# Where the closing steps of the first two elements' attention stand in the issue grid of a four-layer kernel

## Chip, core and metric

The kernel runs on one core of one Trainium2 chip. The metric is the device time of one execution in microseconds (us). Three runs of the kernel before the change took 1100.51, 1100.62 and 1100.92 us.

Five engines are named as the profile names them: PE (matrix engine; PEld is its weight load), DVE (vector engine), ACT (activation engine), POOL (general engine) and SP (which issues all the transfers here). Each engine takes its instructions strictly in the order in which the program lists them, and waits at the first one whose inputs or buffer are not ready.

## What is computed

Four batch elements x[b] of 512 rows by 512 columns go through two decoder layers with gates; g are scalars.

```
x = x + tanh(g_xattn[0]) * wkv(layernorm(x), ctx)        # a scan over the 512 rows, per column
x = x + tanh(g_ffn[0])   * ffn(layernorm(x))             # 512 -> 2048 -> 512, one-bit weights, 8-bit groups
x = x + tanh(g_xattn[1]) * attention(layernorm(x), ctx)  # 16 heads of 32, int8 projections
x = x + tanh(g_ffn[1])   * ternary(layernorm(x))         # rms norm * gamma, 8-bit rows, ternary weight
```

The attention ends, per row, with `out = qdq(o) @ qdq(wp).T + bp`, where qdq rounds a row to 8 bits by its largest magnitude. The ternary layer takes the row's statistics again, scales by gamma, rounds the row to 8 bits by its largest magnitude, and multiplies by a 512x512 ternary matrix. Both are row-wise, so each of the four tiles of 128 rows can be done by itself.

## The kernel before, in words

Rows are cut in four tiles of 128 (t = 0 to 3). Elements are b = 0 to 3 (NB = 4). The four layers of different elements overlap in a pipeline: while element b is in its FFN, element b-1 is in its attention, element b+1 in its scan layer, and the tail of element b-2 (end of attention, ternary layer) is done beside them.

**The order is made by a grid.** Each layer is a Python generator that stops at `yield` after every step. `line(gen, (start, end, steps), ...)` gives it places: a part of n steps is spread evenly from start to end. `run` (L1192, with `place` at L1180) always takes the step with the smallest place next. One element is 1.0 wide and has SLOTS = 17 places, one for each unit of the FFN and a spare; below, "place 6.5" means 6.5/17 of an element behind the beginning of the FFN of element b+2. A line with `aside=True` is put at the integer part of its place plus 0.8. On PE the steps keep this order (`in_turn`, `next_turn`, L147 to L160). On the other engines and SP a scheduler orders the instructions from it, and moves many of them.

**The unit.** One place holds one FFN unit of a row tile (two groups of eight matmuls to `ff_hp`, eight to `ff_acc`, four transposes to `tp_ps`) and one attention unit of a head pair (four `s_ps` matmuls, transposes `pt_ps`, the values `o_ps`, `ot_ps`). On DVE a unit has four row maxima (`at_nm`, L939), the gating (L738, L742), the 8-bit groups (L214, L668, L670, L672), the second halves (L689) and the collection of the head outputs (L991). A chunk of the scan layer adds, every second place, three scans (L591, L621, L626), two reciprocals (L632) and products on POOL (L600, L622, L627, L628, L633, L634).

**What the change moves.** For one row tile, `project_out` (L1008) has three steps: DVE takes the row's largest magnitude (L214) and its scale (L218, L219), and ACT rounds the row (L223); PE transposes it (`qr_ps`, L165) and ACT copies it to `at_oqT` (L230); PE multiplies (`p_ps`, four matmuls), DVE scales the result to `at_y` (L1027), and POOL adds it to `xb` (L1028). The four tiles run staggered by one step, so they take six steps. The ternary layer (L1162) begins with the statistics of all four tiles (L191 to L203, with POOL's power in L180). Per tile, it then centres and scales the row on POOL (`tf_xn`, L211 and L1134), takes its largest magnitude and four short scales on DVE (L214, L1137 to L1145), rounds on ACT (L223), transposes (`qr_ps`, `tf_xT`), multiplies (`f_ps`) and adds on DVE (L1158), and SP stores the rows (L1159): seven staggered steps.

**Buffers in the way.** `at_row` is a ring of three row buffers (ROWS = 3) shared by `at_xn`, `at_q`, `at_half`, `at_y` and `tf_xn`. `m` is three PSUM banks shared by `qr_ps`, `p_ps`, `f_ps`, `pt_ps`, `ot_ps`, `o_ps`, `q_ps`, `tp_ps` and `wy_ps`; `hp` is three banks for `s_ps` and `ff_hp`. The head outputs `at_o` of an element have one buffer, which the next element's attention takes over: its first write (L991) must wait until the last transpose of the element before has read it.

## Time and profile before

| what | value |
|---|---|
| median of three runs | 1100.62 us (1100.51 to 1100.92) |
| the profiled execution: its own time | 1100.92 us |
| the profiled execution: span from first to last instruction | 1099.1 us |
| busy in the span: PE / DVE / ACT / POOL | 939.7 / 831.4 / 726.0 / 314.1 us |
| mean granted PE clock | 0.963 |
| first `ff_acc` of the stretch in which the closing steps of b = 0 stand, and of that of b = 1 | 591.73 and 810.96 us |

The profiled execution's time is 1.8 us more than its span, and 0.3 us more than the median. A unit can be followed in the trace by its group of eight `ff_acc` matmuls; the time from one group to the next is called a unit below. In a row of instructions the columns are start, length, engine, line and operation, and in brackets the idle time of the engine before it and who ended it. A row of a table by stretches gives the stretch and its length, and then, for each engine, its busy time and number of instructions, and at the end the granted PE clock, the transfer engines' busy share and GB/s.

### The profile page before, as it was taken

Reading aid. Unit: us, or ns where it says so; the run is one execution under the profiler, and the core shown is the slowest. Engines: PE = TensorE matmul, PEld = TensorE weight load, DVE = VectorE, ACT = ScalarE, POOL = GpSimd, SP = SyncE. Lnnn points to the kernel's source line nnn. Section 1 sums busy time; section 2 is a strip of 40 time slices with the busy share of each in tenths; the row PEclk is TensorE's granted clock in tenths of the full one; section 3 lists DMA queues with packets and bytes.
Section 4 is the critical chain, followed back from the end, with each engine's and each line's share of the span. In section 5 each row is a group of like instructions: output and inputs, shape, how many; then the busy total and the mean of one; then the engine's idle time right before and its main releaser. Section 6 shows DMA issues by size and latency. Waiting matters only on the chain.

```text
span 1099.1 us, 17965 instructions
## 1 busy us (share of the span) xinstructions
PE 939.7 (85%) x6380; PEld 678.8 (62%) x6380; DVE 831.4 (76%) x1600; ACT 726.0 (66%) x1490; POOL 314.1 (29%) x311
## 2 busy tenths in 40 slices
PE   4879997998888878889998787999998999878885
PEld 2335564565557666667776465777777777656652
DVE  4976548757676789997669988877697765679977
ACT  6656755567345676667767667677685666977863
POOL 3831104422323153531215546422123321100000
PEclk8889999999998999999999999999999999989998
DMA  8178945454344673744755544566455653343411
GB/s 287 39 257 326 323 170 187 147 216 171 136 134 148 233 234 112 252 134 144 230 190 189 168 164 145 172 216 187 173 200 169 208 192 106 83 149 107 116 49 39
DMA packets 85674, 189.68 MB, mean 173 GB/s; under 512 B 12241, under 2 KB 36817, under 8 KB 74577
## 3 DMA queue, kind: packets, MB, share of 16 engines
q1 hardware_dynamic: 85584, 188.53, 51.6%
q8 instruction: 51, 0.84, 0.3%
q14 instruction: 39, 0.31, 0.1%
HBM read 148.65 MB, written 39.85 MB: 171 GB/s over the span
## 4 chain that ended last, share of the span: by engine, by line
PE 45%; DVE 24%; ACT 15%; POOL 7%; issue 7%; DMA 2%; SPq 0%; POOLq 0%; ACTq 0%; DVEq 0%
PE ff_hp L162 14%; PE ff_acc L162 6%; PE pt_ps L165 5%; PE o_ps L162 4%; PE s_ps L162 4%; ACT at_P L941 3%; DVE wk_q L632 3%; PE v_ps L162 3%; ACT at_PT L961 2%; DVE at_nm L939 2%; PE k_ps L162 2%; PE tp_ps L165 2%; DVE wk_p L626 2%; PE qr_ps L165 2%; DVE qg_i L672 1%
## 5 line engine op out<-in xcount | busy, mean ns | idle before, releaser
L162 PE MATMUL ff_hp<-wT,xp 128*128 128x512 f32 x1024 | 270.0, 407 | 3.8 <-ACT at_P L941 2.1
L162 PEld LDWEIGHTS ff_hp<-wT,xp 128*128 128x128 f32 x1024 | 194.2, 193 | 51.3 <-ACT at_P L941 3.8
L941 ACT ACTIVATE at_P<-s_ps,at_nm 128x512 f32<-128x512 f32 x256 | 174.4, 689 | 73.9 <-DVE at_nm L939 70.0
L939 DVE TENSOR_REDUCE at_nm<-s_ps 128x1 f32<-128x512 f32 x256 | 165.5, 676 | 38.0 <-PE s_ps L162 37.3
L677 POOL TENSOR_TENSOR ff_z<-qg_b,qg_s 128x512 f32<-128x512 bf16 x64 | 71.8, 1121 | 334.4 <-ACT qg_b L676 308.3
L165 PE MATMUL pt_ps<-ident,at_P 128*128 128x128 f32 x1024 | 141.1, 278 | 16.4 <-ACT at_os L981 5.4
L961 ACT COPY at_PT<-pt_ps 128x512 f32<-128x512 f32 x224 | 124.3, 595 | 39.6 <-PE pt_ps L165 38.5
L162 PE MATMUL ff_acc<-wT,hr 128*128 128x512 f32 x512 | 137.3, 409 | 4.8 <-ACT hr L688 3.0
L165 PEld LDWEIGHTS pt_ps<-ident,at_P 128*128 128x128 f32 x1024 | 113.2, 140 | 44.4 <-issue 9.1
L162 PE MATMUL s_ps<-at_kR,at_qR 128*128 128x512 f32 x256 | 97.8, 450 | 22.0 <-ACT at_P L941 14.6
L162 PEld LDWEIGHTS ff_acc<-wT,hr 128*128 128x128 f32 x512 | 92.7, 190 | 25.8 <-ACT hr L688 4.0
L737 ACT ACTIVATE ff_z<-ff_hp,coef 128x512 f32<-128x512 f32 x64 | 44.0, 687 | 46.9 <-PE ff_hp L162 44.3
L162 PE MATMUL o_ps<-at_PT,at_V 128*32 128x128 f32 x2048 | 72.2, 279 | 1.3 <-DVE hr L689 0.7
L676 ACT CAST qg_b<-qg_i 128x512 bf16<-128x512 int8 x80 | 49.3, 617 | 31.3 <-DVE qg_i L672 27.4
L742 DVE SCALAR_TENSOR_TENSOR ff_z<-ff_hp,coef,ff_z 128x512 f32<-128x512 f32 x64 | 47.6, 743 | 29.1 <-PE ff_hp L162 29.1
L162 PEld LDWEIGHTS s_ps<-at_kR,at_qR 128*128 128x128 f32 x256 | 45.6, 193 | 38.8 <-ACT at_P L941 23.7
L162 PEld LDWEIGHTS o_ps<-at_PT,at_V 128*32 128x32 f32 x2048 | 53.8, 111 | 23.8 <-issue 11.3
L738 DVE SCALAR_TENSOR_TENSOR ff_z<-ff_z,ff_hp 128x512 f32<-128x512 f32 x64 | 43.4, 678 | 31.4 <-ACT ff_z L737 29.5
L162 PE MATMUL v_ps<-wkvT,cT 128*128 128x512 f32 x128 | 60.9, 622 | 5.7 <-DVE wT L295 2.3
L162 PE MATMUL k_ps<-cT,wkvT 128*128 128x512 f32 x128 | 61.4, 631 | 2.3 <-ACT wk_k L576 1.0
L165 PE MATMUL tp_ps<-ident,ff_z 128*128 128x128 f32 x256 | 40.3, 281 | 23.2 <-ACT at_PT L961 11.0
L632 DVE RECIPROCAL wk_q<-wk_q 128x256 f32<-128x256 f32 x32 | 54.3, 1718 | 1.4 <-POOL wk_p L620 1.4
(178 smaller groups left out, 1664.3 us busy)
## 6 DMA issues: line engine op xcount, KB each, us to landing
wT<-wD SPq DMA_DIRECT2D x72, 1024.0 KB, 5.3
wn<-in_L_ffn_w_dram SPq DMA_DIRECT2D x18, 1024.0 KB, 7.2
at_kR<-kD SPq DMA_DIRECT2D x128, 128.0 KB, 3.0
at_qR<-qD SPq DMA_DIRECT2D x256, 64.0 KB, 2.3
wD<-wT SPq DMA_DIRECT2D x12, 1024.0 KB, 4.2
kD<-k_half SPq DMA_DIRECT2D x16, 512.0 KB, 2.8
qD<-at_half SPq DMA_DIRECT2D x32, 256.0 KB, 2.1
cn<-in_ctx_dram SPq DMA_DIRECT2D x8, 512.0 KB, 6.0
```

What stands on the lines that cost most here:

```text
L162: return in_turn(nc.tensor.matmul(*args, **kwargs))
L165: return in_turn(nc.tensor.transpose(*args))
L626: nc.vector.tensor_tensor_scan(p[:, 1:], A2, E2, 0.0, ALU.mult, ALU.add)
L632: nc.vector.reciprocal(half, half)
L676: nc.scalar.copy(qb, qi)
L677: nc.gpsimd.tensor_tensor(grouped(src), grouped(qb), s.unsqueeze(2).to_broadcast([P, NG, GS]), ALU.mult)
L737: nc.scalar.activation(z, hp, AF.Tanh, scale=coef[:, 0:1])
L738: nc.vector.scalar_tensor_tensor(z, z, 1.0, hp, ALU.add, ALU.mult)
L742: nc.vector.scalar_tensor_tensor(z, hp, coef[:, 1:2], z, ALU.mult, ALU.mult)
L939: nc.vector.tensor_reduce(nm, sp, AX.X, ALU.max, negate=True)
L941: nc.scalar.activation(lanes[k, i, t], sp, AF.Exp, bias=nm, accum_out=sums[k][:, t, i : i + 1],)
L961: made[k] = nc.scalar.copy(dst, blocks(pt))
```

## The change

Two entries of the placing are changed. For every element but b = 2, the six steps that end the attention are spread from `end` to `end + 2.4` places before, and from `end - 0.1` to `end + 3.8` places after. For b = 0 and 1, the seven steps of the ternary layer run from `end + 3` to `end + 8` before, and from `end + 4.1` to `end + 9.1` after.

```diff
             (start, end, 72),
-            (end, end + 2.4 / SLOTS, 6)
+            (end - 0.1 / SLOTS, end + 3.8 / SLOTS, 6)
             if b != NB - 2
             else (end - 0.15 / SLOTS, end + 4.65 / SLOTS, 6),
...
                 late(lambda b=b: ternary_layer(b, xs[b], at)),
-                (end + 3 / SLOTS, end + 8 / SLOTS, 7)
+                (end + 4.1 / SLOTS, end + 9.1 / SLOTS, 7)
                 if b < NB - 2
                 else (end + 4.85 / SLOTS, end + 11.85 / SLOTS, 7),
```

`end` is place 5.95 of the FFN of element b+2. Worked out, the steps stand at these places (the ternary layer's with the rule for `aside`):

| steps | before | after |
|---|---|---|
| end of attention, 6 | 5.95, 6.35, 6.75, 7.15, 7.55, 7.95 | 5.85, 6.5, 7.15, 7.8, 8.45, 9.1 |
| ternary layer, 7 | 8.8, 9.8, 10.8, 11.8, 11.8, 12.8, 13.8 | 10.8, 10.8, 11.8, 12.8, 12.8, 13.8, 14.8 |

For b = 3 nothing else is left to be placed beside these steps. No instruction is added, removed or changed in size.

## Prediction

> **What bounds the kernel here.** I read the table by stretches first, cut at the first `ff_acc` matmul of each unit from place 6.25 on. This is the unit table for the closing steps of b = 0:

> ```profile
> 591.73:613.99 22.26, 16.02 (x104) 11.31 (x105) 20.71 (x33) 16.24 (x33) 14.53 (x13) 0.92 0.73 224
> 613.99:631.92 17.93, 13.60 (x100) 9.86 (x99) 16.96 (x23) 9.88 (x21) 12.16 (x12) 1.00 0.41 146
> 631.92:643.74 11.82, 10.76 (x89) 8.65 (x87) 10.32 (x22) 7.05 (x18) 2.89 (x4) 1.00 0.31 96
> 643.74:659.86 16.12, 12.56 (x88) 9.84 (x87) 14.71 (x30) 11.66 (x22) 8.78 (x8) 0.89 0.58 210
> 659.86:674.58 14.72, 11.20 (x93) 9.09 (x91) 12.99 (x24) 8.97 (x23) 9.74 (x10) 1.00 0.52 163
> 674.58:693.89 19.31, 14.65 (x101) 10.87 (x99) 16.21 (x35) 12.39 (x23) 13.40 (x13) 0.91 0.47 157
> 693.89:706.50 12.61, 11.84 (x96) 9.57 (x95) 11.48 (x24) 9.70 (x25) 3.25 (x3) 1.00 0.33 95
> ```

> Of these 114.8 us PE (first column after the length) is busy 90.6 and DVE (third) 103.4. DVE is the bound, at 90%, and what it lacks, 11.4 us, is waiting. The first two units are long because five of the six closing steps fall into them; the third has no closing step of the attention and takes 11.82.

> The same cut for b = 1, whose neighbour has no scan layer left, shows PE as the bound:

> ```profile
> 810.96:824.20 13.24, 13.24 (x104) 10.21 (x102) 12.93 (x30) 12.28 (x28) 4.81 (x5) 1.00 0.77 266
> 824.20:837.14 12.94, 12.89 (x100) 9.94 (x98) 10.82 (x23) 7.80 (x18) 4.50 (x4) 1.00 0.92 293
> 837.14:850.13 12.99, 10.15 (x84) 8.20 (x83) 9.37 (x26) 7.70 (x21) 4.11 (x4) 1.00 0.07 18
> 871.95:887.53 15.58, 13.07 (x100) 9.77 (x99) 12.63 (x35) 9.09 (x21) 9.82 (x9) 1.00 0.45 138
> ```

> PE idles there only in the last two, 2.84 and 2.51 us. So spreading as such can win nothing: PE's or DVE's work is the same wherever it stands. Only waits can go. DVE's waits between 591.73 and 706.5, longest first:

> ```profile
> DVE tf_s L214 <- POOL tf_xn L1134: 3.4, 3, 1.5
> DVE ln_r L203 <- POOL ln_r L180: 1.8, 2, 1.4
> DVE wk_p L626 <- POOL wk_e L622: 1.4, 2, 0.9
> DVE at_y L1027 <- PE p_ps L162: 1.0, 1, 1.0
> DVE s L191 <- POOL xb L1028: 0.7, 1, 0.7
> ```

> Four of the five are of the moved steps or stand behind them. PE's longest waits in both stretches are effects of a late DVE:

> ```profile
> 609.21 1.11 PE L165 MATMUL qr_ps<-ident,at_o 128*128 128x128 f32 x4 [3.85 <-ACT at_o L223]
> 652.68 1.26 PE L162 MATMUL q_ps<-at_xqT,wqT 128*128 128x512 bf16 x4 [3.56 <-DVE at_o L991]
> 845.36 0.63 PE L165 MATMUL tp_ps<-ident,ff_z 128*128 128x128 f32 x4 [2.84 <-DVE at_o L991]
> ```

> **Part 1, end of attention for b = 0.** The issue order of the changed program puts one closing transposition and product less before the `ff_acc` at 613.99, and two in the unit that had none. In PE's queue the first `qr_ps` now stands behind two `s_ps`, which loses about 0.4 us of cover for the 1.14 us that the second `s_ps` waits at 596.29; DVE's reciprocals (597.39, 3.33 us) end later than that, so it costs nothing. The wait of 3.85 at 609.21 goes, since the row that it transposed is now rounded a unit earlier than needed. What DVE gains of it is only its own two waits, 1.0 (`at_y`) and 0.7 (`s`). One comes new: the last `at_y` (L1027) is now followed after four short rows by the statistics of that tile, which wait for POOL's sum (L1028, 1.29). Queued behind on DVE are the next `ff_acc` result and two row maxima. Sum: -1.7 + 1.3 = **-0.4**. Bounds: -1.7 if other rows fit between, +1.3 if the two old waits only move.

> **Part 2, ternary layer for b = 0.** The wait of L203 on POOL's power (1.4) stays: the order still has both side by side. The three waits on `tf_xn` (3.4) and 0.3 of `at_half` (L895, idle before it at 667.83) belong to a ring: `tf_xn` of tile 0 stands in `at_row` before the rows of the query projection at place 9.75, so the second `at_half` waits until tile 0 is transposed (667.20), POOL's next `tf_xn` waits for L895 (2.12 us idle at 668.75), and DVE waits for POOL at 671.86 (1.47) and 676.21 (0.83). Afterwards the projection's rows come first, and all three `tf_xn` that are queued there follow them; DVE's L214 for tile 0 stands some thirty rows behind L203 instead of five. POOL then needs 3 x (0.77 + 1.28) us while DVE has a scan, two reciprocals (3.3) and six row maxima to do. Sum: **-3.7**. Bounds: 0 (DVE's next row waits instead) to -4.8 (with part of the L622 wait).

> **Part 3, work that leaves the DVE-bound stretch.** Two adds (L1158, 0.73 each) and tile 3's magnitude with four short rows (0.68 + 4 x 0.15) now come behind 706.5: 2.7 us of DVE, at 90% worth 2.4. PE gets with them three transpositions (start to start 0.43) and two products (0.86) in the units of 12.61, 12.83 and 11.39, where it is idle 0.77, 1.13 and 0.22: 3.0 - 2.1 = 0.9 more. Sum: **-1.5**. Bounds: -2.4 to +0.6 (only PE's 3.0 less the 2.4).

> **Part 4, b = 1.** Where PE is full, moving its work one unit on is neutral. The 2.84 wait: DVE waited 1.13 (L203) and 2.27 (L214 behind `tf_xn`) ahead of two row maxima. Now it has 1.2 (statistics behind L1028) and 1.13, and the first `tf_xn` magnitude is a unit later; the matmuls that stand in front (a product, 0.86, and a projection before `tp_ps`) cover some. I leave 1.3 of 2.84: -1.5. The 2.51 at 877 to 882 I leave as they are: the three `tf_xn` chains are as dense as before (POOL 2.05 per tile against 0.9 of DVE between), only a unit earlier, where DVE has more slack (6.60 busy of 10.76) but POOL's queue must first wait for L895.

> **Part 5, a held bank.** `at_o` has one buffer: the next element's first collection (L991) writes it after the last `qr_ps` has read it. Before, that transposition (618.23, and 828.43) came ahead of the first `ot_ps` (620.80, 830.82), so L991 followed at once. Now, in the order, two transpositions come behind `ot_ps`, which keeps its PSUM bank until then, and eight `m` tiles go through two banks. The order shows the consequence: the third `qr_ps` and its product now wait for DVE, that is for the second halves of the `tp_ps` ahead (L689). In b = 1 these ended 2.1 us after their `tp_ps`, with an `at_y` and statistics (1.4) ahead of them that are now gone; I take 1.2 of the 0 to 2.1. In b = 0 I follow PE through the two banks from 612.7 and reach the next `ff_acc` about 4.6 us later than with three, yet still when DVE is ready for it: 0, and 4.6 if DVE were not the later one. Sum with part 4: -1.5 + 1.2 = **-0.3**, from -3.5 to +3.0.

> **Queues passed.** SP: the stores of `out` wait for L1158 (21.5 us in four waits between 570 and 720) with weight loads behind them; two stores now stand together ahead of the load of the last up-weights, which are used some 19 us of PE rows later. Nothing, or one weight load's landing (5.3) if that cover went. POOL: the sums L1028 fall behind products of the scan chunk; their readers are the statistics alone. ACT is busy below 80% in all the units shown but 810.96 (12.28 of 13.24).

> **Ports.** Two of the four L1028 lie beside a lengthened L672 (1.25 and 1.27 against 0.68), the other two beside rows of normal length: 1.2 us of collisions. As many POOL rows run afterwards: I take 0, from -1.2 to +1.2. [...]

> **Sum.** -0.4 - 3.7 - 1.5 - 0.3 = -5.9. Against the profiled execution's 1100.92 (0.3 above the median, inside what repeats differ by) that is **1095.0**. What ends a unit early is kept: nearly everything after 731 is PE-bound with units of 9 to 13 us and no fixed appointments.

> **Rivals.**
> - *The waits move.* POOL's chain for the four ternary tiles is as long as before (8 x about 1 us), and DVE's rows that read it find it late at their new place, so part 2 gives 0 and part 3 half. -0.4 - 0.7 - 0.3 = -1.4: 1099.5. For it: part 4's own case, where the density stays. Against it: DVE's new position, thirty rows behind L203.
> - *The held bank bites (slower).* If DVE turns the two banks over later than PE needs them, the 4.6 of part 5 are on the path in b = 0 and 2.1 in b = 1; it decides as soon as PE's `ff_acc` of place 8.25 ends after DVE wants it, and my margin there is only about 1 us. With half of part 2 and nothing of part 3: +6.7 - 1.9 - 0.4 = +4.4: 1105.3. For it: PE already waits 2.8 us at `tp_ps` behind `at_PT` and 2.8 us at `pt_ps` behind `at_os` in the stretch of b = 0, each for a bank. Against it: there PE is idle 3.5 us per unit, DVE 1.6.
> - *The order doesn't change* is excluded: every engine's list differs in both stretches, and nowhere else.

> **Numbers.** Forecast 0.62, waits move 0.20, held bank 0.18. 0.2% (2.2 us) is about what a measurement of this kernel can tell from no change. Faster by more: 0.61 of the forecast and 0.03 of the first rival, 0.64; within: 0.01, 0.17 and 0.01 of the three, 0.19; slower: 0.17 of the held bank. The range takes the bounds of part 2 to the good side (a further 5 with parts 1 and 4), and to the other goes past the first rival to a held bank that costs half: 1089.5 to 1102.5.

> **What would show it.** Right: no PE wait of 3 us at the `qr_ps` of `at_o`; DVE waits on `tf_xn` of b = 0 under 1 us in all; the stretch from 591.73 to the ninth `ff_acc` after it 5 us shorter; b = 1's stretch within 2 us. Wrong: `tf_s` waits of 3 us again; PE waits at `qr_ps` or `p_ps` on L689 that lengthen the unit at place 7.25; a PE wait at `tp_ps` of 2 us or more near place 9.5 of b = 1.

## The result, and the profile after

The changed kernel takes 1106.26 us (median of four runs, 1105.39 to 1109.16) against 1100.77 us for the kernel before in the same measurement (1100.51 to 1101.92): a ratio of 1.0057, 95% interval 1.0041 to 1.0072. It is slower by 5.5 us where 5.8 us less than the median before were forecast. A second measurement (twelve runs, the last experiment) gives 1.0033, 1.0019 to 1.0046. The profiled execution takes 1106.21 us and has a span of 1104.4 us, 5.3 more than before. Cut at the same `ff_acc` groups, the 5.3 are +0.5 up to 592 (where both kernels issue the same), +1.2 in the ten units of b = 0 (149.77 against 148.55), -0.2 between, +4.1 in the ten units of b = 1 (124.23 against 120.17), and -0.3 behind.

This is the table by units of b = 0 after the change. The first seven rows answer to the seven that the prediction shows; the last three are the units behind them. The last line, from the same table of the kernel before, is the sum of its last three units.

```profile
592.22:610.74 18.52, 13.07 (x95) 9.75 (x97) 18.52 (x29) 13.10 (x29) 12.80 (x12) 1.00 0.69 236
610.74:632.49 21.75, 14.53 (x95) 11.17 (x95) 18.57 (x28) 12.07 (x25) 12.18 (x11) 0.76 0.49 148
632.49:645.58 13.09, 12.82 (x100) 9.88 (x99) 11.88 (x24) 8.64 (x20) 2.64 (x4) 1.00 0.27 92
645.58:660.22 14.64, 12.47 (x87) 9.83 (x87) 12.41 (x24) 9.46 (x18) 6.65 (x7) 0.88 0.49 162
660.22:676.22 16.00, 11.49 (x89) 8.60 (x87) 15.47 (x26) 10.53 (x24) 13.04 (x12) 1.00 0.67 211
676.22:687.64 11.42, 10.55 (x88) 8.61 (x87) 10.07 (x28) 10.36 (x19) 4.73 (x5) 1.00 0.66 224
687.64:705.92 18.28, 13.52 (x104) 10.32 (x103) 16.70 (x30) 11.00 (x26) 12.73 (x11) 1.00 0.29 88
705.92:718.95 13.03, 12.44 (x96) 9.59 (x96) 12.09 (x32) 9.83 (x21) 3.11 (x3) 1.00 0.73 260
718.95:731.27 12.32, 12.05 (x97) 9.56 (x96) 7.11 (x17) 8.12 (x20) 0.50 (x1) 1.00 0.34 87
731.27:741.99 10.72, 9.38 (x81) 6.99 (x79) 7.96 (x17) 7.47 (x18) 3.08 (x3) 1.00 0.73 248
```

```profile
sum 33.78, PE 31.88 PEld 25.37 DVE 25.68 ACT 24.02 POOL 6.68; mean PE 10.63 PEld 8.46 DVE 8.56 ACT 8.01 POOL 2.23
```

The first seven units together take 113.70 us against 114.77, so 1.1 came of the 6.5 that parts 1 to 3 expected there (0.4, 3.7 and 2.4); the last three take 36.07 against 33.78 and give back 2.3. The second unit is the longest of all, at a granted PE clock of 0.76. DVE's waits in the first seven units, longest first, are now these:

```profile
DVE s L191 <- POOL xb L1028: 1.6, 2, 1.4
DVE ff_z L742 <- PE ff_hp L162: 1.5, 2, 0.8
DVE tf_s L214 <- POOL tf_xn L1134: 1.3, 1, 1.3
DVE ln_r L203 <- POOL ln_r L180: 1.1, 1, 1.1
DVE wk_p L626 <- POOL wk_e L622: 1.0, 1, 1.0
```

The waits on `tf_xn` fell from 3.4 to 1.3 (under 1 was forecast), and one on the statistics' sum (L1028) came, as forecast. New are two waits of DVE for PE at L742 (1.5 together); they belong to the new places as such, since e3 below has the same two (0.67 and 0.79). PE itself now has these among its longest waits, the first in b = 0, the others in b = 1:

```profile
624.19 1.11 PE L165 MATMUL qr_ps<-ident,at_o 128*128 128x128 f32 x4 [6.16 <-DVE hr L689]
...
859.02 0.58 PE L162 MATMUL q_ps<-at_xqT,wqT 128*128 128x512 bf16 x1 [2.59 <-ACT at_PT L961]
...
874.06 0.63 PE L165 MATMUL tp_ps<-ident,ff_z 128*128 128x128 f32 x4 [2.73 <-ACT at_PT L961]
```

The first is the held bank of part 5: `ot_ps` (615.85) keeps its bank, both `tp_ps` fill the other two, and the third `qr_ps` of `at_o` waits until DVE has read one of them, behind a scan (2.27 us) and an L672 (1.68 us). DVE then waits twice for the work behind that `qr_ps` (the second time through ACT, which reads `ff_hp`):

```profile
627.05 0.75 DVE L1027 SCALAR_TENSOR_TENSOR at_y<-p_ps,at_s,swp_b 128x512 f32<-128x512 f32 x1 [0.66 <-PE p_ps L162]
...
631.43 0.69 DVE L738 SCALAR_TENSOR_TENSOR ff_z<-ff_z,ff_hp 128x512 f32<-128x512 f32 x1 [0.78 <-ACT ff_z L737]
```

And these are the units of b = 1 to which the two other waits belong, and a later one:

```profile
851.05:865.97 14.92, 12.11 (x88) 9.37 (x87) 10.61 (x25) 7.12 (x16) 4.32 (x5) 0.89 0.40 124
865.97:878.81 12.84, 10.11 (x84) 8.20 (x83) 9.79 (x30) 8.78 (x20) 6.56 (x8) 1.00 0.57 195
902.65:916.11 13.46, 12.12 (x97) 9.59 (x96) 9.51 (x23) 11.34 (x27) 1.05 (x1) 1.00 0.66 209
```

PE idles 2.8, 2.7 and 1.3 us in them, and ran part of the first at half clock.

**A half clock that the prediction left out.** A table by stretches of 2 us around the longest wait shows it (granted PE clock third from the end):

```profile
618.00:620.00 2.00, 0.03 (x1) 0.00 (x0) 0.96 (x3) 0.98 (x3) 2.00 (x2) 0.89 1.02 430
620.00:622.00 2.00, 0.00 (x0) 0.00 (x0) 2.00 (x2) 0.00 (x0) 1.92 (x2) 0.50 0.88 373
...
628.00:630.00 2.00, 2.00 (x6) 1.52 (x5) 2.00 (x3) 1.45 (x4) 1.50 (x3) 0.55 0.00 0
630.00:632.00 2.00, 2.00 (x38) 1.38 (x38) 1.22 (x2) 0.93 (x2) 0.00 (x0) 1.00 0.00 0
```

The clock falls to 0.50 at 619.6 and comes back at 629.8, 5.6 us after the wait has ended. Such stretches stand in every profile of the table below; in before and the change each is 3.41 us long or two, three or four times that (the one that the end of the trace cuts aside). What stood ahead of them is told at the end; here it matters that the same wait may bring one or none (the 2.59 us wait of b = 1 that ends at 859.02 has one beside it here, and the one of 2.59 us that ends at 862.04 in e17 below has none), so every stretch length below stands with their number, counted in pieces of 3.4 us: the one just shown counts as three.

### The profile page after: what moved, and what is told of

Its sections match the earlier page's. It is cut to its first block, busy times and chain, and to the rows that moved or that the text cites. A ratio compares the mean times of both kernels' runs of the same rounds, so it can differ in the third digit from the quotient of the medians.

```text
span 1104.4 us, 17925 instructions
## 1 busy us (share of the span) xinstructions
PE 937.3 (85%) x6348; PEld 678.2 (61%) x6380; DVE 832.9 (75%) x1600; ACT 727.5 (66%) x1490; POOL 314.0 (28%) x311
## 4 chain that ended last, share of the span: by engine, by line
PE 43%; DVE 24%; ACT 16%; issue 7%; POOL 6%; DMA 4%; SPq 0%; POOLq 0%; ACTq 0%; DVEq 0%
PE ff_hp L162 13%; PE pt_ps L165 5%; PE ff_acc L162 5%; ACT at_P L941 4%; PE o_ps L162 4%; PE s_ps L162 4%; DVE wk_q L632 3%; ACT at_PT L961 3%; PE v_ps L162 3%; DVE at_nm L939 2%; PE k_ps L162 2%; PE tp_ps L165 2%; DVE wk_p L626 2%; PE qr_ps L165 1%; DVE qg_i L672 1%
## 5 line engine op out<-in xcount | busy, mean ns | idle before, releaser
L162 PE MATMUL ff_hp<-wT,xp 128*128 128x512 f32 x1024 | 270.1, 407 | 3.1 <-ACT at_P L941 2.1
L162 PEld LDWEIGHTS ff_hp<-wT,xp 128*128 128x128 f32 x1024 | 195.2, 194 | 50.2 <-ACT at_P L941 4.0
L165 PE MATMUL pt_ps<-ident,at_P 128*128 128x128 f32 x1024 | 141.1, 278 | 19.6 <-DVE xb L645 5.0
L961 ACT COPY at_PT<-pt_ps 128x512 f32<-128x512 f32 x224 | 124.2, 595 | 40.7 <-PE pt_ps L165 39.8
L165 PEld LDWEIGHTS pt_ps<-ident,at_P 128*128 128x128 f32 x1024 | 113.2, 140 | 47.6 <-issue 8.5
L162 PE MATMUL ff_acc<-wT,hr 128*128 128x512 f32 x512 | 137.1, 409 | 4.8 <-ACT hr L688 3.0
L162 PE MATMUL s_ps<-at_kR,at_qR 128*128 128x512 f32 x256 | 99.2, 455 | 26.8 <-ACT at_P L941 17.9
L162 PEld LDWEIGHTS ff_acc<-wT,hr 128*128 128x128 f32 x512 | 92.6, 190 | 25.8 <-ACT hr L688 4.0
L162 PEld LDWEIGHTS s_ps<-at_kR,at_qR 128*128 128x128 f32 x256 | 46.0, 195 | 45.3 <-ACT at_P L941 28.0
L162 PE MATMUL o_ps<-at_PT,at_V 128*32 128x128 f32 x2048 | 71.7, 278 | 2.4 <-ACT at_oqT L230 1.7
L742 DVE SCALAR_TENSOR_TENSOR ff_z<-ff_hp,coef,ff_z 128x512 f32<-128x512 f32 x64 | 47.6, 743 | 28.4 <-PE ff_hp L162 28.4
L162 PEld LDWEIGHTS o_ps<-at_PT,at_V 128*32 128x32 f32 x2048 | 53.3, 110 | 24.6 <-issue 11.5
L162 PE MATMUL v_ps<-wkvT,cT 128*128 128x512 f32 x128 | 61.0, 622 | 5.8 <-DVE wT L295 2.3
L162 PE MATMUL k_ps<-cT,wkvT 128*128 128x512 f32 x128 | 62.0, 636 | 2.4 <-ACT wk_k L576 1.0
L165 PE MATMUL tp_ps<-ident,ff_z 128*128 128x128 f32 x256 | 40.8, 284 | 21.8 <-ACT at_PT L961 13.3
```

The lines of the kernel that those rows point to most:

```text
L162: return in_turn(nc.tensor.matmul(*args, **kwargs))
L165: return in_turn(nc.tensor.transpose(*args))
L742: nc.vector.scalar_tensor_tensor(z, hp, coef[:, 1:2], z, ALU.mult, ALU.mult)
L961: made[k] = nc.scalar.copy(dst, blocks(pt))
```

## The experiments

Ratios are to the kernel before in the same measurement, with 95% intervals. The last columns are the ten units of b = 0 and of b = 1 in each run's one profile, with the number of half-clock stretches of 3.4 us in them.

| run | what differs | time, us | ratio | b = 0 | b = 1 |
|---|---|---|---|---|---|
| before | | 1100.77 | 1 | 148.55 (3) | 120.17 (0) |
| the change | both edits | 1106.26 | 1.0057 (1.0041 to 1.0072) | 149.77 (4) | 124.23 (1) |
| e1 | spread alone | 1104.52 | 1.0044 (1.0027 to 1.0062) | 149.83 (6) | 122.86 (0) |
| e2 | ternary placement alone | 1101.42 | 1.0007 (0.9993 to 1.0022) | 146.75 (2) | 122.60 (2) |
| e3 | change, `at_o` in halves | 1103.27 | 1.0022 (1.0008 to 1.0037) | 146.63 (1) | 125.83 (2) |
| e4 | change, sums of b = 1 on DVE | 1101.28 | 1.0009 (0.9994 to 1.0025) | 149.76 (4) | 119.48 (0) |
| e5 | before, sums of b = 1 on DVE | 1098.19 | 0.9973 (0.9958 to 0.9988) | 151.38 (7) | 118.07 (0) |
| e6 | change, halves and sums | 1095.34 | 0.9953 (0.9938 to 0.9968) | 146.67 (1) | 118.84 (0) |
| e7 | e6, gamma of b = 1 on DVE | 1095.71 | 0.9956 (0.9938 to 0.9973) | 148.45 (3) | 118.40 (0) |
| e8 | spread alone, halves | 1098.41 | 0.9980 (0.9968 to 0.9992) | 144.67 (2) | 123.04 (1) |
| e9 | e8, sums of b = 1 on DVE | 1097.82 | 0.9976 (0.9963 to 0.9990) | 144.67 (2) | 122.82 (1) |
| e10 | e9, sums of b = 0 on DVE too | 1100.54 | 0.9997 (0.9984 to 1.0010) | 146.23 (3) | 122.82 (1) |
| e13 | both edits, b = 0 alone | 1101.46 | 1.0001 (0.9987 to 1.0016) | 149.66 (4) | 121.81 (1) |
| e14 | both edits, b = 1 alone | 1103.38 | 1.0015 (0.9998 to 1.0031) | 148.70 (3) | 123.73 (1) |
| e15 | e13, halves, sums of b = 1 | 1094.48 | 0.9936 (0.9914 to 0.9958) | 146.73 (1) | 118.14 (0) |
| e16 | spread of b = 0 alone, halves, sums of b = 1 | 1094.39 | 0.9933 (0.9907 to 0.9960) | 144.44 (4) | 118.08 (0) |
| e17 | the change again | 1104.34 | 1.0033 (1.0019 to 1.0046) | 151.35 (5) | 122.92 (0) |

The number in brackets can be priced from runs whose issue order in a stretch is the same. Before and e5 issue alike until b = 1; the two lines are their ten units of b = 0:

```profile
591.73:740.28 148.55, 122.51 (x907) 94.56 (x908) 129.06 (x245) 99.91 (x209) 71.44 (x64) 0.97 0.53 175
```

```profile
589.57:740.95 151.38, 126.99 (x901) 97.65 (x908) 128.97 (x245) 100.28 (x209) 71.82 (x64) 0.92 0.52 172
```

DVE's work is the same, PE's is 4.5 us longer at a lower clock, and the stretch 2.8 us longer for four half-clock stretches more: 0.7 us each, since DVE bounds b = 0. The price isn't fixed: e9 and e16 issue alike in b = 0 too, and e16, with four stretches, is 0.2 us shorter there than e9 with two. In b = 1, where PE is the bound, before (none) and e13 (one) differ by 1.6 us. A difference of one profile below these sizes says nothing.

**e1, e2: one edit alone.** Each kernel has one of the two hunks of the diff.

> Only the six closing steps of the attention of b = 0 and b = 1 are spread; the ternary layers stay where they were. Two theories of the 5.5 us that the change lost. Held bank: the spread sets the last transpositions of at_o behind the next element's first ot_ps, and the single buffer of at_o then keeps a PSUM bank; PE waits at the third qr_ps (6.2 us in b = 0, 1.1 us in b = 1). By it this kernel alone loses nearly all, 1104 to 1106, and the b = 1 stretch (810.96 to the ninth ff_acc after it, 111.3 us before) is 3 us or more longer. Waits move: what costs is DVE waiting for POOL's rows (L1028 for the statistics, L1134 for the row maxima) at new places; the loss sits mostly in the ternary layers, so this kernel stands within 2 us of before, 1099 to 1103, and its b = 1 stretch within 1.5 us.

> Only the two ternary layers are placed 1.1 places later; the attention ends as before. Held bank: no bank is held here, since every qr_ps of at_o comes before the next ot_ps as before; the kernel stands at before or gains the part of the forecast that the ternary placement was to bring, 1097 to 1101. Waits move: the b = 1 stretch is 2 to 4 us longer than its 111.3, with PE waits of over 2 us behind tf_xn rows of DVE, and the kernel takes 1102 to 1105.

Measured: the spread alone loses 0.44%, the ternary placement alone nothing that the runs can tell. So the held bank's time is met for e1 (1104.5), with the nine units of b = 1 2.7 us longer than their 111.3, a little under the 3 expected. Not all of that is the bank's: e8 below, where the bank is free, still takes 123.04 us for the ten units (one half-clock stretch in it). For e2 the time lies between the two theories, but its b = 1 does what the waits' theory said: nine units 2.4 longer, and one PE wait of 4.40 us at `tp_ps` (867.43), behind the DVE rows for three `tf_xn` (two short rows among them 1.1 and 1.2 us long) that stand ahead of two row maxima. The 7.3 us that PE idles in its ten units are what before had (7.1); what is longer is PE's busy time (115.3 against 113.1), by the two half-clock stretches beside the one long wait. In b = 0, e2's first seven units take 110.69, 4.1 less than before, and its last three 36.06, 2.3 more.

**e3, e8: the held bank taken away.** `at_o` becomes two buffers of two tiles, the same bytes in all; PE's order stays.

```diff
-                pool.tile([P, NT, D], F32, name="at_o", tag="at_o", bufs=1),
+                [pool.tile([P, 2, D], F32, name="at_o", tag=f"at_o{g}", bufs=1) for g in range(2)],
...
-                o_all[:, at : at + 2, p * 64 : p * 64 + 64].rearrange(
+                o_all[at // 2][:, :, p * 64 : p * 64 + 64].rearrange(
...
-            o = o_all[:, t, :]
+            o = o_all[t // 2][:, t % 2, :]
```

> The changed kernel, with at_o as two buffers of two tiles each (the same bytes): the next element's first collection then writes a half whose last transposition is past, so its ot_ps gives its bank back at once. Held bank: the PE waits of 6.2 and 1.1 us at the qr_ps go below 1, and with them the slow clock behind the first; the b = 1 stretch goes from 115.3 to 113 or less and the kernel to 1101 to 1103. Waits move: the PE wait in b = 0 goes, but DVE was busy beside it and nothing is won there; b = 1 wins at most the 1.1; 1104.5 to 1106.

> The kernel before with only the spread of the attention's end, and at_o in two halves. In b = 0 the spread alone cost 1.3 us (149.83 against 148.55) with the bank held. If the held bank is the whole of what the spread does wrong, its ten units of b = 0 take 3 us less than that, 146.5 to 147.5. If the gain in b = 0 comes from the ternary placement alone (146.75 by itself), the spread adds nothing and they take 148 to 149. In b = 1 no repair is made for the statistics' waits, so 121.5 to 123.5 by either.

Measured: with the spread alone the halves turn a loss of 0.44% into a gain of 0.20% (6 to 7 us). The second unit of b = 0, first in e1, then in e8, shows where:

```profile
612.83:634.58 21.75, 14.74 (x96) 11.17 (x95) 18.14 (x27) 12.10 (x25) 12.18 (x11) 0.76 0.47 148
```

```profile
609.93:625.41 15.48, 11.95 (x96) 9.52 (x95) 14.36 (x27) 11.65 (x25) 8.63 (x8) 1.00 0.66 208
```

The same PE instructions take 6.3 us less, DVE leaves 3.8 us of work to the next units, and the clock stays at 1.00; a wait of 2.60 at `p_ps` is what is left of the 6.1. Over the ten units e8 is 5.2 us shorter than e1 and 3.9 shorter than before, below what was expected. On the full change (e3) b = 0 falls by 3.1 and the two waits of DVE at 627.05 and 631.43 are gone, but b = 1 doesn't get shorter as expected (two half-clock stretches in place of one), and the ratio's interval overlaps that of the change measured again. With the sums on DVE besides (e4 to e6) it falls by 0.56%, with intervals apart. So the single buffer of `at_o` costs the spread 3 to 6 us, and DVE being busy beside the wait doesn't hide it.

How much of this is the bank alone isn't shown. Splitting the buffer leaves PE's order as it is, but the scheduler orders DVE anew: in the change the scan L626 stands ahead of the L672 and the two L689 that free the banks, in e3 behind them. The first L689 starts at 623.46 in the change and at 620.66 in e3, and 2.64 us of PE's wait for it are left in e3, at `p_ps`. So most of the difference in this wait is the scan's place in DVE's order. No run holds that order fixed, and none has the halves at the places of before.

**e4, e5: the sums of b = 1 on DVE.** They are on POOL only for b = 0 and 1; the edit takes b = 1 off it.

```diff
-            (nc.vector if b > NB - 3 else nc.gpsimd).tensor_tensor(
+            (nc.vector if b > NB - 4 else nc.gpsimd).tensor_tensor(
                 xb[:, t, :], xb[:, t, :], y, ALU.add
```

> The changed kernel, with the four sums L1028 of b = 1 on DVE in place of POOL (4 x 0.7 us more on DVE, which is busy 70 to 90% of that stretch; the waits of DVE's statistics for POOL, 4.4 us in four, can't arise). Waits move: the PE wait of 2.6 us at q_ps (859.02) and the half clock behind it, 1.5 us, go, so the b = 1 stretch is 3 to 4 us shorter than its 115.3 and the kernel takes 1102 to 1103.5. Held bank: the bank of that q_ps is kept by ot_ps for another reason than the statistics; the stretch moves by less than 1 us, 1105 to 1107.

> The kernel before, with the four sums L1028 of b = 1 on DVE. If what the changed kernel lost in b = 1 is the statistics' waits that the new places made, there is little to win here: the trace of before has one wait of DVE on L1028 in b = 1, 0.7 us, and the b = 1 stretch (ten units from 810.96, 120.2 us) stays within 1 us of that. If the sums on POOL cost wherever they stand (their waits, or POOL's queue that the tf_xn rows share), the stretch falls by 2 us or more, to 118, and the changed kernel's 119.5 with the same edit is then no gain of its own. Time 1099 to 1101 by the first, 1097 to 1099 by the second.

Measured: e4's ten units of b = 1 are 4.7 us shorter than the change's, and its time is 1101.3, both below what was expected. The change's DVE rows ahead of the 2.59 us wait were:

```profile
852.69 1.29 DVE L191 BATCH_NORM_STATS2 s<-xb 128x6 f32<-128x512 f32 x2 [2.05 <-POOL xb L1028]
...
855.59 0.16 DVE L203 SCALAR_TENSOR_TENSOR ln_r<-mv,ln_r 128x4 f32<-128x4 f32 x1 [1.13 <-POOL ln_r L180]
...
856.33 1.28 DVE L939 TENSOR_REDUCE at_nm<-s_ps 128x1 f32<-128x512 f32 x2
...
858.78 0.28 DVE L991 TENSOR_TENSOR at_o<-ot_ps,at_rt 128x128 f32<-128x128 f32 x1
```

Two row maxima stand behind 3.2 us of waiting for POOL, ACT's exponentials and copies behind those, and `q_ps` behind the copies. With the sums on DVE the same units of e4 are:

```profile
848.69:859.74 11.05, 10.92 (x89) 8.62 (x87) 10.70 (x25) 6.97 (x16) 1.50 (x2) 1.00 0.48 146
859.74:871.42 11.68, 10.15 (x84) 8.21 (x83) 9.09 (x26) 7.44 (x19) 8.30 (x9) 1.00 0.68 229
```

14.92 and 12.84 became 11.05 and 11.68; over the ten units DVE has 2.8 us more work (90.5 against 87.7), and PE waits less. For e5 the first theory fails: the kernel before gains 2.1 us in b = 1 and 0.27% too, though DVE waited only 0.7 us for its sums, because POOL, without them, comes earlier to the rows that DVE waits for (2.27 us before `tf_xn` became 0.43) and PE's 2.84 us wait becomes one of 0.76. The sums on POOL are a burden of the kernel, and the change made it larger: moving them wins 4.7 us in b = 1 of the change and 2.1 of before. With the sums on DVE in both, the change is still 1.4 us behind there (e4 against e5).

**e6, e7: both repairs, and gamma on DVE.** e7 has, besides both edits above:

```diff
-            nc.gpsimd.tensor_tensor(xn, xn, gamma_b, ALU.mult)
+            (nc.vector if b > NB - 4 else nc.gpsimd).tensor_tensor(xn, xn, gamma_b, ALU.mult)
```

> The changed kernel with both repairs: at_o in two halves and the sums L1028 of b = 1 on DVE. If the two losses are separate, the ten units of b = 0 take 146.6 (as with the halves alone) and those of b = 1 119.5 (as with the sums alone), together 2.6 us less than before's 148.55 and 120.17, and the time is 1097 to 1098.5 against 1100.4. If the halves' longer b = 1 (125.8 against 124.2) was more than the chance of where the half-clock stretches fell, b = 1 stays above 120.5 and the time above 1099.

> As the run with both repairs, and also the ternary layer's products by gamma (L1134) of b = 1 on DVE: 4 x about 1 us more there, and POOL's part of each tf_xn is one row of 0.77 in place of two of 2.05 together. If DVE's waits for tf_xn (2.56 and 2.52 in the run with the sums alone) are what PE's remaining 1.5 and 1.3 us wait for, both go and the ten units of b = 1 take 117 to 118.5. If PE waits there for a PSUM bank whatever DVE waits for, or DVE's added 4 us stand in its way, they take 119 to 121.

Measured: the repairs are separate and add up in the stretches (146.67 and 118.84); the time is about 2 us below what was expected, and the changed kernel with them beats the kernel before by 0.47%. With gamma on DVE b = 1 takes 118.40, 0.4 less and within what was expected, but PE's waits don't go (1.35 and 1.04 us), DVE now waits 3.0 us for POOL's other row of `tf_xn` (L211), and the time is the same.

**e9, e10: without the ternary placement; all sums on DVE.** e9 is e8 with e4's edit; e10 has `b >= 0` in place of `b > NB - 4`.

> The spread of the attention's end alone, the ternary layers as before, at_o in two halves, and the sums L1028 of b = 1 on DVE: the change without the part that the runs so far show as a loss beside the spread (with the halves, the ternary placement took the time from 1098.4 to 1103.3). If each of these stands for itself, the ten units of b = 0 take 144.7 as in the run with halves and spread (give or take 0.8 for each half-clock stretch of 3.4 us more or less), those of b = 1 118 to 119, and the time is 1093 to 1095, below every kernel so far. If the ternary placement is what keeps b = 1 short once the sums are on DVE, b = 1 takes 120 or more and the time is 1096 to 1098.

> The same with the sums L1028 of b = 0 on DVE too. DVE is the bound there: four rows of about 0.75 us are 3.0 us more. If POOL's sums cost DVE as much in waits for the statistics (1.6 us in two waits in the changed kernel) and in rows lengthened beside POOL's, the ten units of b = 0 stay within 1 us of the run with the sums of b = 1 alone. If DVE's work is all that counts, they are 2.5 to 3.5 us longer.

Measured: e9's b = 0 comes as expected, its b = 1 doesn't: 122.82, with a PE wait of 3.05 (875.65) and one half-clock stretch. So with the sums on DVE the two edits need each other in b = 1 (both: 119.48 in e4, 118.84 in e6), and without either (e5: 118.07) it is best. A likely reason is that the ternary layer's steps, not moved on, come at once behind the last sum; no run tests it. In e10, 3.0 us more DVE rows in b = 0 cost 1.6 us, of which 0.7 is one half-clock stretch more: by this profile about two thirds of the rows' length are repaid elsewhere in the stretch. By the medians e10 is 2.7 us slower than e9, nearly the whole length; which of the two holds stays open.

**e11, e12: four banks for `m`.** The banks are divided `{"m": 4, "hp": 2, "acc": 2}` in place of 3, 3, 2, with the spread alone (e11) and with the places of before (e12).

> The spread alone, with at_o as it was, and the PSUM banks divided 4, 2, 2 in place of 3, 3, 2 (tag m one more, tag hp one less): a held bank then leaves three. It stands beside the kernel before with the same banks. If the spread loses because ot_ps keeps one of three banks, PE's wait of 6.1 us at the third qr_ps goes without any change of at_o, and the spread costs nothing or gains up to 2.5 us against the kernel before with the same banks. If the wait on at_o itself (the order of reader and writer) is what costs, the wait stays and the spread loses 3 to 5 us here too.

> The kernel before with the PSUM banks divided 4, 2, 2: the control of the run before. ff_hp has two banks in place of three, one of which each of its two halves in flight needs; I expect 1098 to 1108, and use only the difference of the two.

Measured: 1281.4 and 1292.2 us (1.164 and 1.1735 times before). The control is far outside its expectation: with two banks for `ff_hp` and `s_ps`, PE waits 172.9 us in 82 waits at `ff_hp` (e11). The spread is 0.8% ahead there, and no `qr_ps` of `at_o` waits over 1.3 us for one tile, which agrees with a held bank. But the kernel is bound elsewhere, so I don't rest the price on it.

**e13 to e16: one element at a time, and the best of each.** The edits get `if b == 0` or `if b == 1`; e15 and e16 add halves and e4's sums.

> Both edits of the change, for b = 0 alone. By the profiles (b = 0 +1.2 us) the time is 1.2 us above before, 1101 to 1102.5. If the wait of 6.2 us and the half-clock stretches that it can bring weigh more on the average of runs than in the one profile, as the 3.0 us that the halves brought there suggest, 1103 to 1104.

> Both edits for b = 1 alone. By the profiles (b = 1 +4.1 us, one half-clock stretch in it) the time is 4 us above before, 1104 to 1105.5. If b = 0 carries more than its profile showed, this one is 1102 to 1103.5. The two runs' differences to before should add up to the change's 5.5.

> Both edits for b = 0 alone, at_o in two halves, the sums L1028 of b = 1 on DVE, b = 1 placed as before. From the stretches measured so far: b = 0 146.6 (before 148.55), b = 1 118.1 (before 120.17): 4.0 us below before, 1096 to 1097.5. If the ternary placement of b = 0 hurts beside the spread, this is 1.5 us or more above the next run; if it helps, below it.

> The same without the ternary placement: only the spread of b = 0's closing steps, halves, sums of b = 1 on DVE. b = 0 144.7, b = 1 118.1: 6.0 us below before, 1094 to 1095.5. If the gain of b = 0 in the two profiles with halves and spread alone was the luck of the clock, 1096.5 to 1098.

Measured: b = 0 alone costs nothing that the runs can tell, b = 1 alone 0.15%, with an interval that just reaches no change. e15 and e16, which have b = 0's spread with halves and b = 1 left in its places, are 0.64 and 0.67% faster than before and the same as each other in time. So the ternary placement of b = 0 neither helps nor hurts there, though their profiles differ by 2.3 us in b = 0. These two have the lowest times here; their intervals overlap those of e6 and e7.

**e17: the change again.**

> The changed kernel once more. If the shares of b = 0 and b = 1 add up (0.01% and 0.15%), it stands 0.1 to 0.3% above before here, 1102 to 1104. If the two edits lose something together that neither element shows alone, 0.5% or more, 1105.5 to 1107. In the trace the stretch of b = 0 is 149.8 with four half-clock stretches and 0.75 us longer or shorter for each more or less, that of b = 1 122.5 plus about 1.65 for each.

Measured: 0.33%, between the two expectations. The shares of e13 and e14 (0.16% together) lie below its interval, but within what their own intervals leave room for; the 0.57% of the first four runs may have been high. The trace again has the 6.2 us wait; b = 1, without a half-clock stretch this time, takes 122.92: 2.75 us more than before from waits alone (PE is busy 113.1 us in both).

## Why the prediction was wrong, step by step

- **Part 5, the held bank, is the step that failed most.** It saw the bank held, the third `qr_ps` waiting for L689, and 4.6 us for it in b = 0, but put it at 0 because PE would still be ready "when DVE is ready for it". PE waited 6.2 us, and splitting `at_o` is worth 3.1 us in that stretch (149.77 to 146.63) and 0.56 to 0.64% in time (e4 to e6, e1 to e8). Neither engine covers the other there: PE waits for DVE's L689, which stands behind a scan, and DVE then waits for the PE work behind that `qr_ps` (0.66 and 0.78 us, both gone in e3), which in addition runs at half clock (0.50 until 629.8). For b = 1 the 1.2 us were right (1.07 measured at 832.66).
- **Part 4, b = 1.** "I leave 1.3 of 2.84" expected PE to be covered behind the statistics. Two sums were awaited at once (2.05 us), then POOL's power (1.13), with two row maxima behind: 2.59 us of PE and a half-clock stretch. The waits on `tf_xn` came out nearly as said, 2.73 us of PE for 2.51, and a further 1.29 came behind them. Parts 4 and 5 said -0.3 for this element; +4.1 was measured. Of that 1.3 is the half-clock stretch (e17, without one, has 2.75), 1.3 more goes when the sums leave POOL (3.4 from e17 to e4, less the 2.1 that before gains too), and 1.4 stays, with the 1.07 at 832.66 in it.
- **Part 3, -1.5.** It counted on 2.7 us of DVE work going behind 706. By the traces one add (0.7) and one row of statistics (0.7) with a few short rows went, about 1.5 in all; tile 3's magnitude stays ahead (676.21 before, 701.40 after). Nor did DVE get shorter ahead of 706: 103.6 us busy for 103.4, since about as much came by lengthening, net of a few rows that got shorter: the seven L672 from 1005 to 1119 ns each, the four L637 from 874 to 1153 ns, the one L895 from 751 to 1778 ns. The long ones among these overlap a POOL row that was already running (L895 at 657.24, POOL's L627 from 656.88 to 658.47; the L672 of 1.68 us at 621.85, POOL's L628 from 620.93 to 622.99; the L637 of 1.77 us at 668.55, POOL's L600 from 668.49 to 669.77); none of the long L672 lies beside one of the L1028 that **ports** counted, and its "I take 0" was too low. (Of the two that it counted, the L672 at 627.13 began while POOL's L600 was running, and only the one at 606.48 beside an L1028.) Behind 706 the sum left 0.9 for PE, counted from 693.89 on. The last three units alone take 2.3 more in every kernel with b = 0's moved layer (36.1, and 37.13 in e17 with a half-clock stretch; 33.8 without): PE has 2.0 us more work there, and its idle time (0.59, 0.27, 1.34 us) is no shorter than before.
- **Part 2, -3.7, was right in its sum and partly by luck.** e2, which has this part alone with part 3, wins 4.1 ahead of 706, of which 0.7 is one half-clock stretch less; DVE's idle time there falls from 11.4 to 7.4. But the terms are others: the waits on `tf_xn`, which were to go, fell only from 3.4 to 2.4, and those of L203 on POOL's power (1.8), which were to stay, went. The gain was spent as above.
- **Part 1** held in its mechanism: the 3.85 us wait went and the new one on L1028 came (1.39 for 1.29). Its 1.0 at `at_y` stayed in the change (0.66 and 0.26) and goes where `at_o` is split. There the spread, with the split, is worth far more than the -0.4 of this part: e8's b = 0 is 3.9 us shorter than before's, with one half-clock stretch less.
- **What no part had**: the half clock. In e2's b = 1, with two half-clock stretches beside one 4.40 us wait, PE was busy 115.3 us against 113.1 in before, which has two shorter waits there and no such stretch. The half clock also put into both kernels' single profiles differences as large as most of the terms.

The rival "the held bank bites" (1105.3) came within 1 us of both measurements and named the right PSUM banks and, with part 5, the right `qr_ps`. Its total is near partly by luck: its 2.1 for b = 1 is 1.1, and the statistics' waits there are not in it. The 5.3 us of the two profiles go back to the single buffer in b = 0 (3.1, e3), the units behind 706 (2.3) and b = 1 (4.1, divided above), less what parts 1 and 2 won. Left open: why the medians give the halves about 6 us where the profiles' stretches give 3 to 5 (the half clock doesn't explain it in b = 0: in all five profiles with the hold there, the wait is 6.1 to 6.2 us and draws three half-clock stretches), how much of the halves' gain is DVE's new order, and how the change's 0.3 to 0.6% divides exactly between the elements.

## What to carry to other kernels

Where steps are moved past the next element's first write, look up which buffer the moved step reads last and what that write holds while it waits: here a single-buffered result kept a PSUM bank, and splitting the buffer in two, at no cost in bytes, turned the spread alone from a loss of 0.44% into a gain of 0.20%. A wait that another engine's work "covers" is covered only if nothing of that engine's next work depends on the waiting one. Where the granted clock falls to 0.50 behind waits, as it did here, count the half-clock stretches before comparing one profile's stretch with another's, and judge by the median of many runs.

## What the runs showed of the hardware

The raster's place also fits part of the scatter of runs. Before and the change issue alike up to 592 us. The group of `ff_acc` that comes at 468.62 us in before comes at 467.50 in the change, with 14 half-clock windows ahead of it where before has 16. The next group, with the 2.90 us wait ahead of it that brings a half-clock window in the change alone, comes at 482.37 and at 482.82: this unit is 1.57 us longer in the change.
